# Attention and mixture of experts on one core: which unit the planner calls next, and how three quarters of the outputs are added up

## The chip, the core and the metric

The kernel runs on one core of one Trainium2 chip, and everything is float32. The time is the device time of one execution in microseconds (us). The kernel before took 654.52 us, the median of three runs (654.38 to 657.39). Engines are named as the profile names them: PE for matmuls (PEld for the loading of their weights), DVE, ACT, POOL and SP. Each has an in-order queue of its own.

## The reference, cut to what matters

The input x has 4 x 1024 tokens of 256 channels. The output is x plus two branches that both read the layer-normalised x:

```
xn = layernorm(x)
x + attention(xn) + ffn(xn)

# attention: 16 heads of 16 channels
local  = causal linear attention(q, k, v), chunks of 128 tokens
fine   = sum over 4 memories, weighted by a softmax over the batch's mean queries
coarse = one summed memory
memory = p * fine + (1 - p) * coarse          # p from a small gate on coarse
output = (gate * memory + (1 - gate) * local) @ w_o.T

# ffn: 8 experts of width 176, two for each token, and a shared one of width 352
scores = softmax(x @ gate_weight.T); the two largest, normalised
y = sum over the token's two experts of weight * (silu(x @ wg.T) * (x @ wu.T)) @ wd.T
y = y + shared(x)
```

## The kernel before

**Tiles.** The 4096 tokens are 32 tiles of 128 rows (`NTT` = 32), in blocks of 4 tiles (`NT` = 4). A *round* n does the attention of tile n on PE: `scores`, `memory`, `local`, `back`, `update`, `turned`, `gate_hidden`, and for tile n - 2 `output`, which adds the shared expert's second half and the projection by `w_o` in one PSUM bank. Beside the rounds run the projections and the shared expert of later blocks, and the routed experts: a sort of the tokens by expert fills 71 slot tiles (`NST` = 71) of 128 rows each. For each slot tile j, POOL gathers its rows from DRAM (`fetch_rows`, L1133, tile `xg`), SP loads the expert's weights (`fetch_weights`), PE transposes the rows (`expert_turn`, `pte`, L1166), does the two halves of the expert (`expert_hidden`, `phe`, L1183, and `expert_out`, `pye`, L1215), ACT scales the result (`expert_y`, tile `y`, L1224) and POOL scatters it with an adding indirect DMA (`put`, L1229) onto `sums`, an array in DRAM with a row for each token, which starts as a copy of x (L1615). Any `put` can touch any row, so each waits until the one before it has landed.

**The end of an output.** `held_from` is 24. For tiles 24 to 31, `output` comes last in the program: their rows of `sums` are loaded by `residual` (L1055), DVE adds them to the bank (`output_sum`, L1083), and ACT's queue stores them one at a time (`store_one`). For tiles 0 to 23, `output` comes in the rounds, ACT copies the bank to SBUF (`output_copy`, L1089, tile `acc`), and the rest waits for the last `put`: twelve loads of two tiles each from `sums` on SP's queue (`experts_part`, L1099, tile `part`), twelve additions on POOL (`total`, L1113) and twelve stores on SP's queue (`store_two`, L1117).

**The planner.** The order of the instructions is written by a list scheduler in the kernel's own Python (`plan`, L1357 on). It keeps a queue of units for each function, a table `cost` with each unit's engine and an assumed duration, `needs`, which names the units that one waits for, and `lag` and `landing`, the assumed time from a unit's end until its result can be used. It walks through time: of all units whose inputs are planned, each engine's candidate is the one that can begin first; the earliest over the engines is called next. On PE, among units that can begin equally early, the one that is due first goes:

```
            rank = (begin, due if engine == "PE" else ready)
```

`batch_weights` (L689 on) makes a softmax over the memories once for each of the four batches: two small matmuls (`pr`, L695), then some dozen short DVE instructions with one on ACT (L700 to L719). The table books it as 3.50 us of PE and nothing on DVE.

Of the kernel before, what the change touches and what calls it, by code (L numbers as in the profile page):

```python
# [8 lines left out]
FP = mybir.dt.float32  # L9
I32 = mybir.dt.int32  # L10
AF = mybir.ActivationFunctionType
ALU = mybir.AluOpType
AX = mybir.AxisListType

P = 128
NT = 4
TB = P * NT
# [5 lines left out]
def linear_attention_moe_kernel(  # L23
# [28 lines left out]
    nc = tc.nc  # L52
    T, H = x.shape
# [3 lines left out]
    NC = H // P  # L57
# [667 lines left out]
    def at(n):  # L725
        blk, i = divmod(n, NT)
        return blk, i, slice(i * P, (i + 1) * P)
# [360 lines left out]
        blk, i, _ = at(n)  # L1088
        nc.scalar.copy(st["acc", blk][:, i, :], st.pop(("po", n))[:, :H])  # L1089

    def experts_part(n):

        if n < 3 * NT:
            if n % NT == 0:
                st["parts"] = big.tile([P, NT, VW], FP, tag="tok", name=f"part_{n}")
            res = st["parts"][:, n % NT : n % NT + 2, :H]
        else:
            res = in_weights(n)
        nc.sync.dma_start(  # L1099
            res, sums[n * P : (n + 2) * P, :].rearrange("(n p) h -> p n h", p=P)  # L1100
        )
        st["part", n] = res

    def in_weights(n):
        tag, parts = ("wgu", [P, NC, 2, F]) if n % 4 else ("wdn", [P, 2, H])
        flat = "p a b c -> p (a b c)" if n % 4 else "p a b -> p (a b)"
        res = exw.tile(parts, FP, tag=tag, name=f"part_{n}").rearrange(flat)
        return res[:, : 2 * H].rearrange("p (n h) -> p n h", h=H)

    def total(n):  # L1110
        blk, i, _ = at(n)
        acc = st["acc", blk][:, i : i + 2, :]
        nc.gpsimd.tensor_add(acc, acc, st.pop(("part", n)))  # L1113

    def store(n, tiles, queue):
        blk, i, _ = at(n)
        queue.dma_start(  # L1117
            out[n * P : (n + tiles) * P, :].rearrange("(n p) h -> p n h", p=P),
            st["acc", blk][:, i : i + tiles, :],
        )  # L1120

    def store_two(n):
        store(n, 2, nc.sync)

    def store_one(n):
        store(n, 1, nc.scalar)


    def fetch_rows(j):
# [227 lines left out]
    def plan(order):  # L1357
# [12 lines left out]
            scores: ("PE", 1.10), memory: ("PE", 0.85), local: ("PE", 1.05), back: ("PE", 0.92),  # L1370
            update: ("PE", 0.48), turned: ("PE", 0.45), keys_back: ("PE", 0.45),
            output: ("PE", 2.17), gate_hidden: ("PE", 0.47), project: ("PE", 1.73),
            shared_gate: ("PE", 1.73), shared_up: ("PE", 1.73), batch_weights: ("PE", 3.50),
            expert_turn: ("PE", 0.24), expert_hidden: ("PE", 1.36), expert_out: ("PE", 0.95),
            odd_keys: ("ACT", 0.52), turned_copy: ("ACT", 0.57), keys_copy: ("ACT", 0.62),
            output_copy: ("ACT", 0.40), local_copy: ("ACT", 0.60), gate_out: ("ACT", 0.90),
# [3 lines left out]
            gate_sum: ("DVE", 0.50), blend: ("POOL", 0.78), weigh_local: ("DVE", 1.08),  # L1380
            state: ("DVE", 0.43), projected: ("DVE", 0.74), shared_silu: ("DVE", 0.66),
            shared_hidden: ("DVE", 0.66), expert_silu: ("DVE", 1.00), mean_queries: ("DVE", 1.30),
            gate_coarse: ("POOL", 0.78), sum_fine: ("POOL", 2.80), base: ("POOL", 0.78),
            add_state: ("POOL", 0.80), put: ("POOL", 1.62), fetch_rows: ("POOL", 1.02),
            fetch_weights: ("SP", 0.3), invert: ("DVE", 1.15), hold: ("ACT", 1.00),
            hold_weights: ("POOL", 0.72), add_slots: ("PE", 0.75), inverted: ("DVE", 0.65),
            residual: ("SP", 2.0), experts_part: ("SP", 1.0), output_sum: ("DVE", 0.45),
            total: ("POOL", 1.4), store_two: ("SP", 1.0), store_one: ("ACT", 0.1),
        }

        lag = {"PE": 0.22, "ACT": 0.06, "DVE": 0.06, "POOL": 0.06, "SP": 4.0}
        landing = {fetch_rows: 2.0, put: 2.9, residual: 2.5, experts_part: 2.5}
        batch = batches[1] - batches[0]

        def key_of(f, args):
# [2 lines left out]
        def needs(f, n, *more):  # L1398
# [8 lines left out]
                scores: lambda: qs + ks + [(odd_keys, n), (fine, n - 1, NC - 1)],  # L1407
                mask: lambda: [(scores, n), (local, n - 1)],
                memory: lambda: [(mask, n, g) for g in range(NG)],
                weigh: lambda: [(memory, n), (turned, n - 2), (gate_coarse, n - 1)],  # L1410
                gate_coarse: lambda: [(weigh, n), (base, n - 1), (sum_fine, n - 1)],
                fine: lambda: [(weigh, n), (sum_fine, n - 1)],
                sum_fine: lambda: [(fine, n, NC - 1), (gate_coarse, n), (gate_out, n - 2)],
# [20 lines left out]
                + [(shared_hidden, blk, f) for f in range(NF)],  # L1434
                output_copy: lambda: [(output, n)],
                output_sum: lambda: [(output, n), (residual, n - n % NT)],
                residual: lambda: [(put, NST - 1), (residual, n - NT)],
                experts_part: lambda: [(residual, NTT - NT)],
                total: lambda: [(experts_part, n), (output_copy, n), (output_copy, n + 1)],
                store_two: lambda: [(total, n)],  # L1440
                store_one: lambda: [(output_sum, n)],

                invert: lambda: [(add_slots, n - 3 * batch)],
                hold: lambda: [(invert, n), (add_slots, n - 3 * batch)],
# [28 lines left out]
                expert_silu: lambda: [(expert_tanh, n), (expert_out, n - 2)],  # L1473
                expert_out: lambda: [(expert_silu, n)],
                expert_y: lambda: [(expert_out, n), (put, n - 3)],
                put: lambda: [(expert_y, n), (put, n - 1)],
            }[f]()


# [22 lines left out]
        def longest_free(ring):  # L1502

            slots = [(-1.0 if u is None else called[u], k)
                     for k, u in enumerate(rings[ring]) if u is None or u in called]
            return min(slots)[1] if slots else None
# [3 lines left out]
        def add(f, args, due):  # L1510
            queues.setdefault(f, []).append((key_of(f, args), args, due, place))

        for w, f, *args in order:

            if f is end:
                ended = True
            if f not in cost:
                continue
            if not ended:
                place = due  # L1520
            add(f, args, due)
            if f is project:
                add(project_exp, [args[0], *args[2:]], due)
            elif f is fine and args[1] == NC - 1:
                add(sum_fine, args[:1], due)
            elif f is expert_turn:
                if args[0] + 2 < NST:
                    add(fetch_rows, [args[0] + 2], due)
                if args[0] + 1 < NST:
                    add(fetch_weights, [args[0] + 1], due)  # L1530
            if not (f is update and args[0] % (BPB * NT) == last_of_batch):
                for g in after.get(f, ()):
                    if f is output and args[1]:
                        g = output_sum
                    add(g, args[:1] if f is output else args, due)
            if cost[f][0] == "PE":
                due += cost[f][1]
        known = {op[0] for queue in queues.values() for op in queue}
        queues = {f: queue[::-1] for f, queue in queues.items()}
        free = dict.fromkeys(lag, 0.0)  # L1540
        done, called = {}, {}
        window = 12.0
        while any(queues.values()):
            limit = window + min(
                (q[-1][3] for f, q in queues.items() if q and cost[f][0] == "PE"), default=0.0
            )
            best = {}
            for f, queue in queues.items():
                if not queue:
                    continue  # L1550
                key, args, due, place = queue[-1]
                engine = cost[f][0]
                if engine == "PE" and place > limit:
                    continue
                waits = [key for key in needs(*key) if key in known]
                takes = taken(f, key)
                if takes:
                    slot = longest_free(takes[0])
                    if slot is None:
                        continue  # L1560
                    waits += [rings[takes[0]][slot]]
                if any(w is not None and w not in done for w in waits):
                    continue
                ready = max((done[w] for w in waits if w is not None), default=0.0)
                begin = max(ready, free[engine])
                rank = (begin, due if engine == "PE" else ready)
                if engine not in best or rank < best[engine][0]:
                    best[engine] = rank, f
            assert best
            rank, f = min(best.values(), key=lambda b: b[0][0])  # L1570
            begin = rank[0]
            key, args, *_ = queues[f].pop()
            engine, took = cost[f]
            takes = taken(f, key)
            if takes:
                rings[takes[0]][longest_free(takes[0])] = takes[1]
            called[key] = len(called)
            if f is update and (state, *key[1:]) not in known:
                took = 0.0
                done[add_state, *key[1:]] = begin  # L1580
                called[add_state, *key[1:]] = len(called)
            free[engine] = begin + took
            done[key] = begin + took + landing.get(f, lag[engine])
            f(*args)


# [91 lines left out]

    order += [(0, end)] + [u for n in range(last_round, NTT + 2) for u in rounds[n]]
    order += [(10, residual, n) for n in range(held_from, NTT, NT)]  # L1680
    order += [(10, experts_part, n) for n in range(0, held_from, 2)]
    for n in range(0, held_from, 2):
        order += [(64, total, n), (10, store_two, n)]
    order += [u for pair in shared(NBLK - 1) for u in pair if u]
    for n in range(held_from, NTT):
        order += [(1280, output, n, True), (10, store_one, n)]
    planned.append(True)
    plan(order)

# [55 lines left out]
```

## Time and profile before

The profiled execution took 651.07 us; the span from its first to its last instruction is 649.4 us.

| what | value |
|---|---|
| median of the runs, lowest and highest | 654.52, 654.38, 657.39 us |
| profiled execution, its span | 651.07, 649.4 us |
| granted PE clock, mean | 0.998 |
| busy share: PE, PEld, DVE, ACT, POOL | 97%, 75%, 66%, 43%, 63% |
| adding scatters, L1229: count, mean, share of POOL | 71, 1585 ns, 112.6 us |
| gathers of rows, L1133: count, mean | 71, 1006 ns |
| additions at the end, L1113: count, mean | 12, 1222 ns |

"Busy" is the time in which an engine's instructions were under way. A matmul is pipelined, so PE can be busy and still have small holes. A row of waits names the engine and line that waited, who released it, then the total, the number of times and the longest in us. In a timeline the columns are start, length, engine, line, operation, and in square brackets the engine's idle time before it with what ended it.

### The profile page before, as it was taken

To read this page: it belongs to the slowest core of one execution; us is meant where nothing else is said; L and a number is where in the kernel's file an instruction comes from. 1 tells how busy PE (TensorE), PEld (TensorE's weight loads), DVE (VectorE), ACT (ScalarE), POOL (GpSimd) and SP (SyncE) were. 2 spreads that over 40 slices of the span, in tenths; PEclk is the share of its full clock that TensorE was granted. 3 is DMA by queue.
4 is the path that set the end of the run, shared out by engine and by line. 5 is a ranking of instruction groups with operands and counts; after the bars stand their busy time and mean duration, and the time that the engine had idled before them with its cause. 6 is when DMAs were issued, how large, how long until landed. Compare 5 with 4: busy or idle time off the path is not lost.

```text
span 649.4 us, 15187 instructions
## 1 busy us (share of the span) xinstructions
PE 627.6 (97%) x5510; PEld 487.9 (75%) x5510; DVE 429.5 (66%) x1205; ACT 278.5 (43%) x676; POOL 408.6 (63%) x456
## 2 busy tenths in 40 slices
PE   4999999989999999999999999999999999999996
PEld 3884467778888877777786777788888886778775
DVE  6837999966665566566656765666655656667751
ACT  3765455444444454334533444333445434344320
POOL 5310055677777876565665665677777498586876
PEclk9999999999999999999999999999999999999999
DMA  9779000156566753443443444346666675564278
GB/s 301 242 238 248 0 1 2 50 168 166 133 152 144 164 129 87 106 107 77 109 118 78 106 107 98 89 106 138 154 151 160 149 161 127 147 164 99 26 225 301
DMA packets 94379, 86.51 MB, mean 133 GB/s; under 512 B 12033, under 2 KB 91905, under 8 KB 94177
## 3 DMA queue, kind: packets, MB, share of 16 engines
q1 hardware_dynamic: 78976, 65.34, 34.5%
q0 software_dynamic: 13632, 18.62, 16.6%
q10 hardware_dynamic: 1696, 1.58, 0.7%
q8 instruction: 44, 0.72, 0.5%
q14 instruction: 31, 0.25, 0.1%
HBM read 67.56 MB, written 23.59 MB: 140 GB/s over the span
## 4 chain that ended last, share of the span: by engine, by line
PE 89%; DVE 6%; ACT 1%; DMA 1%; issue 1%; POOL 0%; DVEq 0%
PE phe L1183 14%; PE pye L1215 11%; PE po L1071 6%; PE psu L1030 6%; PE pg L1010 5%; PE quad L746 5%; PE pn L772 5%; PE pv L407 5%; PE po L1075 4%; PE quad L889 4%; PE pq L649 3%; PE pk L649 3%; PE pte L1166 3%; PE pb L793 2%; PE pb L799 2%; PE found L617 2%
## 5 line engine op out<-in xcount | busy, mean ns | idle before, releaser
L1229 POOL DMA_INDIRECT sums<-y,islot x71 | 112.6, 1585 | 56.5 <-ACT y L1224 16.1
L1183 PEld LDWEIGHTS phe<-turned,wgu 128*128 128x128 f32 (+1 forms) x852 | 102.2, 187 | 14.9 <-issue 12.9
L1183 PE MATMUL phe<-turned,wgu 128*128 128x128 f32 (+1 forms) x852 | 108.0, 276 | 0.0
L1133 POOL DMA_INDIRECT xg<-xns,islot x71 | 71.4, 1006 | 58.0 <-PE pte L1166 43.9
L753 DVE TENSOR_TENSOR sT<-quad,causal 128x512 f32<-128x512 f32 x128 | 79.4, 682 | 21.9 <-PE quad L746 9.5
L1215 PE MATMUL pye<-wdn,hidden 112*128 112x256 f32 (+1 forms) x284 | 77.9, 396 | 0.5
L1200 DVE SCALAR_TENSOR_TENSOR the<-the,phe 128x256 f32<-128x256 f32 x71 | 29.5, 415 | 43.3 <-ACT the L1195 30.0
L1215 PEld LDWEIGHTS pye<-wdn,hidden 112*128 112x128 f32 (+1 forms) x284 | 48.8, 190 | 11.4 <-issue 3.2
L936 POOL TENSOR_TENSOR fm<-fm 128x512 f32<-128x512 f32 x32 | 48.2, 1506 | 4.2 <-DVE fm L923 4.2
L1224 ACT ACTIVATE y<-pye,wslot 128x256 f32<-128x256 f32 x71 | 33.4, 471 | 38.9 <-PE pye L1215 36.2
L1195 ACT ACTIVATE the<-phe 128x256 f32<-128x256 f32 x71 | 27.1, 382 | 51.6 <-PE phe L1183 45.8
L608 POOL TENSOR_TENSOR held<-ones,two 128x213 f32<-128x213 f32 (+1 forms) x22 | 16.3, 748 | 49.5 <-DVE ones L581 49.5
L1071 PE MATMUL po<-wd,h 128*128 128x256 f32 (+1 forms) x192 | 47.0, 380 | 0.0
L1010 PE MATMUL pg<-xnT,wg 128*128 128x512 f32 (+1 forms) x96 | 45.7, 598 | 0.5 <-DVE th L1040 0.5
L1030 PE MATMUL psu<-xnT,wu 128*128 128x512 f32 (+1 forms) x96 | 45.9, 600 | 0.0
L923 DVE TENSOR_TENSOR fm<-quad,rw 128x512 f32<-128x512 f32 x64 | 41.0, 682 | 0.2
L1071 PEld LDWEIGHTS po<-wd,h 128*128 128x128 f32 (+1 forms) x192 | 35.5, 190 | 6.1 <-issue 1.6
L916 POOL TENSOR_TENSOR cg<-coarse,gates 128x256 f32<-128x256 f32 x32 | 30.9, 964 | 13.9 <-DVE coarse L904 11.6
L1173 ACT COPY turned<-pte 128x256 f32<-128x256 f32 x71 | 26.5, 373 | 27.6 <-PE pte L1166 25.6
L1002 POOL TENSOR_TENSOR o<-o,loc 128x256 f32<-128x256 f32 x32 | 29.7, 929 | 7.8 <-ACT o L996 5.8
L772 PE MATMUL pn<-sT,va 128*32 128x128 f32 x1024 | 34.6, 276 | 0.0
L827 POOL TENSOR_TENSOR loc<-loc,cg 128x256 f32<-128x256 f32 x32 | 26.5, 827 | 12.7 <-DVE loc L817 12.0
(200 smaller groups left out, 1329.8 us busy)
## 6 DMA issues: line engine op xcount, KB each, us to landing
wdn<-in_w_down_dram SPq DMA_DIRECT2D x71, 224.0 KB
wgu<-in_w_gate_dram SPq DMA_DIRECT2D x71, 176.0 KB
wgu<-ups SPq DMA_DIRECT2D x71, 176.0 KB
xns<-x SPq DMA_DIRECT2D x8, 512.0 KB
sums<-in_x_dram SPq DMA_DIRECT2D x8, 512.0 KB
x<-in_x_dram SPq DMA_DIRECT2D x7, 512.0 KB
part<-sums SPq DMA_DIRECT2D x12, 256.0 KB
out_dram<-acc SPq DMA_DIRECT2D x12, 256.0 KB
```

The costliest lines, as they stand in the source:

```text
L649: nc.tensor.matmul(pq, w[:, k, c * P : (c + 1) * P], xnT[:, k, :], start=(k == 0), stop=(k == NC - 1),)
L753: nc.vector.tensor_mul(sT, quad[:, g, :].rearrange("p (c t) -> p c t", t=P), causal[:, None, :].to_broadcast([P, NC * 2, P]),)
L772: nc.tensor.matmul(pn[CW * r : CW * (r + 1), q, :], wide[:, i, first : first + CW], st["sT", h // 2][:, c * 2 + h % 2, :], start=True, sto ...
L923: nc.vector.tensor_mul(fm[:, c].rearrange("p g m (r k) -> p g (m r) k", k=HD), quad[:, :, c * KM + KX + KN : (c + 1) * KM].rearrange("p g ...
L936: nc.gpsimd.tensor_add(fm[:, :, 0:2, :], fm[:, :, 0:2, :], fm[:, :, 2:4, :])
L1010: nc.tensor.matmul(pg[:n, :], wg[:, k, f * P : f * P + n], xnT[:, k, :], start=(k == 0), stop=(k == NC - 1),)
L1030: nc.tensor.matmul(pu[:n, :], wu[:, k, f * P : f * P + n], xnT[:, k, :], start=(k == 0), stop=(k == NC - 1),)
L1071: nc.tensor.matmul(po[:, :H], st["h", blk, f][:k, tok], wd[:k, f, :], start=(f == 0), stop=False)
L1133: nc.gpsimd.indirect_dma_start(out=xg, out_offset=None, in_=xns, in_offset=bass.IndirectOffsetOnAxis(ap=islot[:, j : j + 1], axis=0),)
L1183: nc.tensor.matmul(ph[: cols.stop - cols.start, s, :], wgu[:, k].rearrange("p g f -> p (g f)")[:, cols], xgT[:, k, :], start=(k == 0), sto ...
L1215: nc.tensor.matmul(py[:, :H], hT[:n, f, :], wdn[:n, f, :], start=(f == 0), stop=(f == 1))
L1229: nc.gpsimd.indirect_dma_start(out=sums, out_offset=bass.IndirectOffsetOnAxis(ap=islot[:, j : j + 1], axis=0), in_=st.pop(("y", j)), in_of ...
```

## The change

The change has two parts, both in the functions above.

**The planner.** For PE, a unit is no longer ranked by when its inputs are planned to be ready, but by that time plus a margin by the engine that makes the input (`spare`: ACT 0.4, DVE 0.6, POOL 1.5, SP 1.0 us); the unit's due time decides among units that are past the margin. The time at which a unit is booked now counts all its inputs and the buffer that it takes. `batch_weights` is booked with 0.95 us of PE, and DVE is held for a further 2.2 us after it, and `weigh` waits for it. `sum_fine` is booked with 3.20 us rather than 2.80.

**The outputs of tiles 0 to 23.** `experts_part`, `in_weights`, `total` and `store_two` are gone. After each odd tile's `output_copy`, `join` adds two tiles of `acc` onto their rows of `sums` by one adding DMA of 256 KB from POOL's queue. It takes its turn with the `put`s, one landed before the next begins. After the last one, six copies of 512 KB from `sums` to `out` (`copy_out`, SP's queue, DRAM to DRAM) take the place of the twelve loads and twelve stores.

```diff
-    def experts_part(n):
...
-    def in_weights(n):
...
-    def total(n):
+    def join(n):
+
         blk, i, _ = at(n)
-        acc = st["acc", blk][:, i : i + 2, :]
-        nc.gpsimd.tensor_add(acc, acc, st.pop(("part", n)))
-
-    def store(n, tiles, queue):
+        nc.gpsimd.dma_start(
+            sums[n * P : (n + 2) * P, :].rearrange("(n p) h -> p n h", p=P),
+            st["acc", blk][:, i : i + 2, :],
+            accum_op=ALU.add,
+        )
+
+    def copy_out(blk):
+        rows = slice(blk * TB, (blk + 1) * TB)
+        nc.sync.dma_start(out[rows, :], sums[rows, :])
+
+    def store(n):
         blk, i, _ = at(n)
-        queue.dma_start(
-            out[n * P : (n + tiles) * P, :].rearrange("(n p) h -> p n h", p=P),
-            st["acc", blk][:, i : i + tiles, :],
-        )
-
-    def store_two(n):
-        store(n, 2, nc.sync)
-
-    def store_one(n):
-        store(n, 1, nc.scalar)
+        nc.scalar.dma_start(out[n * P : (n + 1) * P, :], st["acc", blk][:, i, :])
...
-            shared_gate: ("PE", 1.73), shared_up: ("PE", 1.73), batch_weights: ("PE", 3.50),
+            shared_gate: ("PE", 1.73), shared_up: ("PE", 1.73), batch_weights: ("PE", 0.95),
...
-            gate_coarse: ("POOL", 0.78), sum_fine: ("POOL", 2.80), base: ("POOL", 0.78),
+            gate_coarse: ("POOL", 0.78), sum_fine: ("POOL", 3.20), base: ("POOL", 0.78),
...
-            residual: ("SP", 2.0), experts_part: ("SP", 1.0), output_sum: ("DVE", 0.45),
-            total: ("POOL", 1.4), store_two: ("SP", 1.0), store_one: ("ACT", 0.1),
+            residual: ("SP", 2.0), copy_out: ("SP", 0.3), output_sum: ("DVE", 0.45),
+            join: ("POOL", 1.2), store: ("ACT", 0.1),
...
-        landing = {fetch_rows: 2.0, put: 2.9, residual: 2.5, experts_part: 2.5}
+        landing = {fetch_rows: 2.0, put: 2.9, join: 3.8, residual: 2.5}
...
-                weigh: lambda: [(memory, n), (turned, n - 2), (gate_coarse, n - 1)],
+                weigh: lambda: [
+                    (memory, n), (batch_weights, n // (BPB * NT)), (turned, n - 2), (gate_coarse, n - 1)
+                ],
...
-                put: lambda: [(expert_y, n), (put, n - 1)],
+                put: lambda: [(expert_y, n)],
...
+        serial = (put, join)
+        free = dict.fromkeys([*lag, "rows"], 0.0)
+        done, called, by = {}, {}, {}
+
+        spare = {"PE": 0.0, "ACT": 0.4, "DVE": 0.6, "POOL": 1.5, "SP": 1.0}
...
-                begin = max(ready, free[engine])
-                rank = (begin, due if engine == "PE" else ready)
+                begin = max(ready, free[engine], free["rows"] if f in serial else 0.0)
+                rank = (begin, ready)
+                if engine == "PE":
+                    safe = max((done[w] + by.get(w, 0.0) for w in waits if w), default=0.0)
+                    rank = (max(begin, safe), due)
...
             free[engine] = begin + took
+            if f in serial:
+                free["rows"] = begin + took + landing[f]
             done[key] = begin + took + landing.get(f, lag[engine])
+            by[key] = spare[engine]
+            if f is batch_weights:
+                free["DVE"] = max(free["DVE"], done[key]) + 2.2
+                done[key] = free["DVE"]
             f(*args)
...
     order += [(10, residual, n) for n in range(held_from, NTT, NT)]
-    order += [(10, experts_part, n) for n in range(0, held_from, 2)]
-    for n in range(0, held_from, 2):
-        order += [(64, total, n), (10, store_two, n)]
+    order += [(10, copy_out, blk) for blk in range(held_from // NT)]
```

## The prediction

> **What bounds the kernel now.** I read the page first, then the waits of PE, then the timeline where PE waits, and last the windows of the end.
>
> ```profile
> PE 627.6 (97%) x5510; PEld 487.9 (75%) x5510; DVE 429.5 (66%) x1205; ACT 278.5 (43%) x676; POOL 408.6 (63%) x456
> ...
> L1229 POOL DMA_INDIRECT sums<-y,islot x71 | 112.6, 1585 | 56.5 <-ACT y L1224 16.1
> ...
> L1133 POOL DMA_INDIRECT xg<-xns,islot x71 | 71.4, 1006 | 58.0 <-PE pte L1166 43.9
> ```
>
> PE is the bound: 97% of the span, and the chain that ended last is 89% PE. The change leaves every matmul as it is, so it can win only the time in which PE waits, and the time after PE's last matmul. The waits of PE:
>
> ```profile
> PE pt L385 <- ACT x L367: 8.7, 2, 7.6
> PE pb L793 <- ACT nT L784: 2.4, 2, 1.2
> PE pte L1166 <- DMA xg<-xns,islot: 2.2, 2, 1.4
> PE pte L1166 <- issue: 1.1, 1, 1.1
> PE pg L1010 <- DVE th L1040: 0.5, 1, 0.5
> PE pk L838 <- ACT oc L965: 0.3, 1, 0.3
> ```
>
> 8.7 us are the first load and normalisation, which the change doesn't touch. The rest, with two rows of 0.2 us, comes to 6.9 us in 640. Holes shorter than about 0.15 us aren't in this list. The Trainium skill ("Trainium Kernel Development and Optimization", Performance Expectations) calls matmul busy time a bad metric because matmuls are pipelined; so I don't take 6.9 us as all that could be won, and allow some 3 us more below the view's limit.
>
> The end, in windows (us, length, busy time of PE, PEld, DVE, ACT and POOL with instructions, granted clock, DMA share, GB/s):
>
> ```profile
> 625.00:635.00 10.00, 10.00 (x49) 8.40 (x48) 2.81 (x8) 1.38 (x4) 8.18 (x10) 1.00 1.09 352
> 635.00:645.00 10.00, 8.97 (x42) 7.53 (x40) 2.12 (x5) 0.00 (x0) 8.42 (x8) 1.00 1.08 379
> 645.00:650.00 5.00, 0.00 (x0) 0.00 (x0) 0.00 (x0) 0.00 (x0) 0.00 (x0) 0.68 0.26 91
> ```
>
> Two things fill these 20 us: PE without a hole, and the DMA engines, full at 352 to 379 GB/s. The last addition on DVE ends at 644.43 and the last store is issued at 644.73, so 4.6 us of the span lie behind that issue.
>
> **The end of the outputs.** Gone are 12 loads and 12 stores of 256 KB (6.3 MB) and the 12 additions (L1113, 14.2 us of POOL). None of it is on the path: PE is busy beside it to 644. The six copies move 3.1 MB. The trace has such copies: the eight of 512 KB that fill `sums` (L1615), in a window from 44 to 58 us with DMA share 1.00 at 316 GB/s. So 3.1 MB take about 10 us. They stand behind the two loads of residuals, which the last scatter releases at 621.5; 1 MB at 350 GB/s is 3 us, so they land near 635 to 636, nine us before the last store. They pass no instruction that anyone waits for: SP has nothing else left.
>
> What is won is only that the last 128 KB store finds free DMA engines. In the row of waits at the end SP waits 3.8 us for stores to land. How long one takes alone: the last scatter, as large, ends on POOL at 617.81 + 1.59 = 619.40, and SP's load that waits for its landing goes out at 621.51, so 2.1 us with the DMA share at 0.18. From 644.73 + 0.34 to about 648.6 the store took 3.5. The gain lies between 0 and 1.4; I take **0.8**, as a store's first bytes may be no earlier than the scatter's.
>
> **The joins.** Twelve adding DMAs go onto POOL between 134 and 600 us, where POOL is busy 324.6 of 466 us. The trace has none of this form. The gather (1006 ns, 128 rows of 1 KB, no addition) bounds the cost from below; twice the scatter (2 x 1585 = 3170 ns, for 256 rows) from above. The nearest row is the scatter, also an addition from SBUF to `sums`; the join has twice its rows but no indices. I take 1.6 us, so 12 x 1.6 = 19 us, and POOL goes from 70% to 74%. Behind a waiting join stand, in the order of the changed program, the next blend or gate (`o`, `cg`), whose transposes PE needs, and the next gather. The series of scatters: 71 x (1.59 + 2.1) = 262 us of the 472 between the first and the last; twelve joins of about 1.6 + 2.6 (landing scaled for twice the bytes) add 50, so the series has room. Cover is POOL's idle 30%; I cost the joins at nothing. Without cover a join costs PE what exceeds the planner's 1.2 us and its margin of 1.5.
>
> A rule speaks against them: "SBUF — State Buffer" (the box on "DVE blocks DMA") says that POOL cannot write its descriptors while DVE runs a two-port operation; a DMA of 620 ns then takes 3100. By it the joins would cost 12 x 3.1 = 37 us of POOL, and the excess over 2.7 would reach PE. The row decides: the 71 scatters take 1563 / 1586 / 1641 ns (lowest, median, highest) beside a DVE that is busy 64% of that stretch. Nothing there is blocked that way.
>
> **The planner.** The waits by cause:
>
> - *The softmax.* Timeline at 338 to 345:
>
> ```profile
> 338.09 0.22 DVE L700 COPY rel<-pr 128x64 f32<-128x64 f32 x1 [2.59 <-PE pr L695]
> ...
> 340.58 0.28 DVE L719 COPY w<-alive 128x8 f32<-128x8 f32 x1
> ...
> 343.48 0.41 DVE L1200 SCALAR_TENSOR_TENSOR the<-the,phe 128x256 f32<-128x256 f32 x1
> ...
> 344.62 0.41 PE L1166 MATMUL pte<-ident,xg 128*128 128x128 f32 x2 [1.07 <-issue]
> ```
>
> The softmax holds DVE from 338.09 to 340.86, 2.8 us that the old plan books on PE (3.5, against 0.5 measured) and not on DVE. So DVE comes to the expert's product (L1200) 2.7 us after ACT gave its input (340.40 + 0.38), and PE waits 1.1 us for a bank. With 2.2 us booked on DVE most of this goes: **-1.1**.
>
> - *nT to pb, 2.4 us.* By the order of the changed program and the rows' durations, the PE work between `local` and `back` of one tile goes from 1.32 to 1.72 us in the median (shortest: 0.90 to 1.19). 0.4 us more margin covers part. But in one case (ACT idle for 3.2 us before `nT` at 533.56, though PE's matmul had started at 530.1) the lateness isn't the plan's. I take half, **-1.2**.
>
> - *The first gathers, 2.2 us.* They get worse. From the last matmul of the sort (128.0) to the first transpose (134.16) it is 6.2 us. Before, an output, `memory`, `gate_hidden` and `local` lie between: 2.2 + 0.8 + 0.4 + 1.1 = 4.5 us. In the changed order only `scores`, `turned` and an output: 1.1 + 0.4 + 2.2 = 3.7. And `expert_hidden` of tile 0 follows straight on its transpose, so PE also waits for ACT's copy (0.37, about 0.7 with its signals); the second transpose then finds its rows there (0.8 won). In sum 0.8 + 0.7 - 0.8 = **+0.7**.
>
> - *The small ones*, 0.5 + 0.3 + 0.2 + 0.2 = 1.2 us: half goes, **-0.6**. And of the some 3 us below the view's limit a third, **-1.0**.
>
> What is late next is the same kind of thing at other places; the halves allow for that.
>
> **The sum.** -1.1 - 1.2 + 0.7 - 0.6 - 1.0 = -3.2, with the end -4.0 us. The profiled execution took 651.07 us, so its like would take 647.1. The median of the runs lies 3.45 us above it, which no view explains, and I leave that as it is: 654.5 - 4.0 = **650.5 us**. Since what can be told from no change is about 0.5%, 3.3 us, the limit is 651.2.
>
> **Rivals.**
>
> *More is won.* The margins take away nearly all listed waits but the first gathers (6.9 - 2.2 = 4.7), all 3 us below the limit, and the end gives 1.0: 654.5 - 8.7 + 0.7 = 646.5. For it: no unit pair in the changed order is closer than its chain needs, except the first expert. Against it: part of the waits isn't the plan's.
>
> *No change.* A new order moves waits rather than removing them; only the end's 0.8 stays: 653.7. For it: the plan's gaps differ from before in most rounds; the expert's two halves stand nearer (a tenth of them within 4.1 us of PE work, before 5.2). Against it: the softmax was booked wrongly, and now isn't.
>
> *Slower: POOL.* Place: the blends and gathers behind a join. If a join holds POOL for 3.2 us, it exceeds 1.2 + 1.5 = 2.7 by 0.5, and each of twelve delays PE by that: +6, so 654.5 - 4.0 + 6.0 = 656.5. It decides from about 2.7 us a join. For it: twice the rows, one landing to wait for, and tensor operations on POOL stretch already (L936 from 1.27 to 1.84 us). Against it: POOL's longest waits are its own, 43.9 us for PE at the gathers.
>
> That the change doesn't do what it says is ruled out: the program has 12 adding DMAs on POOL and 6 copies on SP, and as many matmuls as before.
>
> **How the numbers follow.** Forecast 0.42 (648 to 652.5), more won 0.14, no change 0.22, slower 0.22. Of the forecast's 0.42, 0.36 lie below 651.2. Faster 0.36 + 0.14 = 0.50, same 0.06 + 0.22 = 0.28, slower 0.22. The range goes from a little below the second case to a little above the slower one's 656.5: 645.5 to 657.
>
> **What would show it.** Right: PE's list without the 1.1 us of issue near 344 and with about 1.2 for `nT`; 2.5 to 3 us at the first `pte`; the join's row at 1.3 to 2 us; the DMA engines quiet from 636; under 4 us from the last store to the end. Wrong: a join over 2.7 us, PE waits on `o`, `cg` or `xg` just behind joins, or a sum of PE's waits that is no smaller while other names stand in it.

## The result, and the profile after

The changed kernel took 657.6 us in the median of 20 runs (654.26 to 660.66), the kernel before 654.45 beside it. The ratio is 1.0038, with a 95% interval of 1.0022 to 1.0054: a little slower, 7 us above the forecast of 650.5 and 0.6 us outside its range. Measured twice more (E9 and E13 below), the ratio was 1.0086 (1.0053 to 1.012) and 1.0032 (1.0016 to 1.0049). The profiled execution took 657.98 us with a span of 656.3 and a mean granted clock of 0.992.

The rows of the page that answer to those shown of before:

```profile
PE 630.9 (96%) x5510; PEld 489.2 (75%) x5510; DVE 432.0 (66%) x1205; ACT 278.8 (42%) x676; POOL 412.4 (63%) x456
...
L1209 POOL DMA_INDIRECT sums<-y,islot x71 | 112.8, 1588 | 58.4 <-DMA sums<-y,islot 14.4
...
L1113 POOL DMA_INDIRECT xg<-xns,islot x71 | 72.3, 1018 | 42.1 <-PE pte L1146 29.5
```

(From here on a line of the changed program is 20 lower than that of the same code before.) The same matmuls now keep PE busy for 630.9 us instead of 627.6, and the share falls from 97% to 96%: PE is slower *and* waits more. The waits of PE say where:

```profile
PE pt L385 <- ACT x L367: 9.1, 2, 8.0
PE pte L1146 <- DMA xg<-xns,islot: 3.8, 1, 3.8
PE pt L950 <- POOL o L1002: 3.1, 1, 3.1
PE po L1071 <- DVE hidden L1185: 1.6, 1, 1.6
PE phe L1163 <- PE pte L1146: 0.9, 1, 0.9
```

`nT` and the 1.1 us of issue near 344 are gone, as forecast. In their place stand two waits of over 3 us, each at one place. The windows around the two (columns as before; each ends where the granted clock can change, see below) show what comes with them:

```profile
136.01:139.43 3.42, 1.20 (x6) 0.71 (x4) 1.42 (x3) 0.37 (x1) 2.93 (x5) 1.00 0.57 168
139.43:142.84 3.41, 1.41 (x5) 1.04 (x6) 0.00 (x0) 0.37 (x1) 3.10 (x3) 0.50 0.40 115
142.84:146.25 3.41, 3.41 (x25) 3.08 (x27) 0.72 (x3) 0.76 (x2) 1.73 (x3) 0.50 0.81 118
231.59:235.00 3.41, 0.50 (x5) 0.50 (x6) 1.77 (x8) 0.35 (x1) 2.53 (x3) 1.00 0.64 138
235.00:238.40 3.40, 3.40 (x7) 1.32 (x6) 2.29 (x4) 0.58 (x1) 2.52 (x3) 0.50 0.66 145
```

The granted clock falls to 0.50 late: at 139.43, when PE has waited for 2.2 us and will wait for 1.5 more, and at 235.00, half a microsecond after the second wait has ended. It stays there for 6.8 and for 3.4 us, most of them full of work. In the profiled execution of before it was full from the warm-up to the last matmuls.

**The first gathers.** POOL's timeline, from the additions in front to the first gathers, then PE's:

```profile
133.34 1.27 POOL L936 TENSOR_TENSOR fm<-fm 128x512 f32<-128x512 f32 x1
...
136.90 0.72 POOL L827 TENSOR_TENSOR loc<-loc,cg 128x256 f32<-128x256 f32 x1
137.80 1.23 POOL L1113 DMA_INDIRECT xg<-xns,islot  x1 [0.18 <-issue]
```

```profile
132.95 0.41 PE L617 MATMUL found<-held,ones 128*128 128x142 f32 x2
...
136.18 1.03 PE L1075 MATMUL po<-wo,oc 128*128 128x256 f32 x4
140.97 0.66 PE L1146 MATMUL pte<-ident,xg 128*128 128x128 f32 x2 [3.77 <-DMA xg<-xns,islot]
142.09 2.93 PE L1163 MATMUL phe<-turned,wgu 128*128 128x128 f32 x12 [0.46 <-ACT turned L1153]
```

The same two places before:

```profile
127.76 0.41 PE L617 MATMUL found<-held,ones 128*128 128x142 f32 x2
...
134.16 0.41 PE L1166 MATMUL pte<-ident,xg 128*128 128x128 f32 x2 [1.44 <-DMA xg<-xns,islot]
```

DVE made `islot`, the row numbers that the gathers need, at 134.68 + 0.23 = 134.91, but in POOL's queue six additions stand ahead of the gather, from `o` at 132.66 to `loc`, and it starts 2.9 us later. From the sort's last matmul to the first transpose it is 8.0 us (140.97 - 132.95), before 6.4 (134.16 - 127.76). PE has 4.2 us of work in between. Then twelve matmuls of `phe` take 2.93 us; at full clock they take 1.49.

**The blend at 231 us.** POOL, then PE, then POOL's blend before:

```profile
225.70 1.59 POOL L1209 DMA_INDIRECT sums<-y,islot  x1 [0.25 <-issue]
...
230.79 1.59 POOL L1209 DMA_INDIRECT sums<-y,islot  x1 [0.31 <-issue]
232.68 1.01 POOL L1113 DMA_INDIRECT xg<-xns,islot  x1 [0.31 <-issue]
233.71 0.74 POOL L1002 TENSOR_TENSOR o<-o,loc 128x256 f32<-128x256 f32 x1
235.57 1.30 POOL L1094 DMA_DIRECT2D sums<-acc  x1 [1.13 <-DMA sums<-y,islot]
```

```profile
234.50 0.44 PE L950 MATMUL pt<-ident,o 128*128 128x128 f32 x2 [3.07 <-POOL o L1002]
...
234.99 3.58 PE L649 MATMUL pk<-xnT,wk 128*128 128x512 f32 x4
```

```profile
225.19 0.74 POOL L1002 TENSOR_TENSOR o<-o,loc 128x256 f32<-128x256 f32 x1
```

ACT delivered `o` at 226.73. POOL's blend of it starts at 233.71, behind three additions, a memset, a scatter and a gather. Before, the same blend came at 225.19 and PE did not wait. No join stands in this stretch of POOL's queue (the last one was issued at 197.74), so this trace alone doesn't say that the joins are the cause.

**The joins and the end.** A join takes 1300 / 1314 / 1392 ns of POOL (lowest, median, highest). How long a scatter takes to land in mid-kernel can be read where the next one waits for it, here in the trace of before:

```profile
210.16 1.58 POOL L1229 DMA_INDIRECT sums<-y,islot  x1 [2.03 <-DMA sums<-y,islot]
...
215.42 1.57 POOL L1229 DMA_INDIRECT sums<-y,islot  x1 [0.90 <-DMA sums<-y,islot]
```

The first landed 5.26 - 1.58 = 3.7 us after its end on POOL. The end of the changed kernel in windows:

```profile
635.00:645.00 10.00, 10.00 (x52) 8.81 (x51) 2.65 (x8) 2.03 (x6) 2.44 (x4) 1.00 1.00 371
645.00:650.00 5.00, 5.00 (x25) 4.38 (x24) 0.85 (x2) 0.00 (x0) 0.00 (x0) 1.00 0.20 71
```

The DMA engines are full while the six copies run and nearly idle from 645 on, 8 us before PE's last matmul, which ends at 653.2. From PE's last matmul to the end it is 3.2 us, before 5.4.

### The profile page after: what moved, and what is told of

Same layout as the page of the kernel before. It is cut to its first block, busy times and chain, and to the rows that moved or that the text cites. A ratio compares the mean times of both kernels' runs of the same rounds, so it can differ in the third digit from the quotient of the medians.

```text
span 656.3 us, 15167 instructions
## 1 busy us (share of the span) xinstructions
PE 630.9 (96%) x5510; PEld 489.2 (75%) x5510; DVE 432.0 (66%) x1205; ACT 278.8 (42%) x676; POOL 412.4 (63%) x456
## 3 DMA queue, kind: packets, MB, share of 16 engines
q10 hardware_dynamic: 1696, 1.58, 0.7%
## 4 chain that ended last, share of the span: by engine, by line
PE 83%; DVE 9%; POOL 2%; ACT 2%; issue 2%; DMA 1%; another core or an unknown queue 0%; DVEq 0%; POOLq 0%; ACTq 0%
PE phe L1163 14%; PE pye L1195 10%; PE po L1071 6%; PE psu L1030 5%; PE pg L1010 5%; PE quad L746 5%; PE pv L407 5%; PE pn L772 4%; PE po L1075 4%; PE quad L889 3%; PE pk L649 3%; PE pq L649 3%; PE pte L1146 2%; PE found L617 2%; PE pt L950 2%
## 5 line engine op out<-in xcount | busy, mean ns | idle before, releaser
L1163 PE MATMUL phe<-turned,wgu 128*128 128x128 f32 (+1 forms) x852 | 109.7, 279 | 1.4 <-PE pte L1146 0.9
L916 POOL TENSOR_TENSOR cg<-coarse,gates 128x256 f32<-128x256 f32 x32 | 27.4, 855 | 15.7 <-DVE coarse L904 11.6
L827 POOL TENSOR_TENSOR loc<-loc,cg 128x256 f32<-128x256 f32 x32 | 30.0, 937 | 6.1 <-DVE loc L817 5.5
```

The source lines that it names most:

```text
L1163: nc.tensor.matmul(ph[: cols.stop - cols.start, s, :], wgu[:, k].rearrange("p g f -> p (g f)")[:, cols], xgT[:, k, :], start=(k == 0), sto ...
```

## The experiments

Ratios are to the kernel before, measured in the same call; in brackets the 95% interval. Chips and hours differ by some us (the kernel before had medians from 651.5 to 655.7 us), so times are compared only within a call.

**E1 to E4: which half of the change makes which wait?** E1 is the changed planner with the old outputs; E2 the old planner with the joins and copies; E3 leaves the plan and drops the calls; E4 widens the planner's view.

```diff
# E3, in plan:
-            f(*args)
+            if f is not join:
+                f(*args)
# E4, in plan:
-            limit = window + min(
+            limit = (window if (expert_turn, 0) in called else 24.0) + min(
```

> The changed planner alone, with the outputs as they were before (loads, additions and stores at the end, no joins). Theory 'margins': the new rank itself leaves PE without work at the first gathers (its own plan has a gap of 2.96 us before the first expert's transpose, the old plan has none), and a PE wait of over 3 us halves the granted clock for some us. Then the wait of 3 to 4 us at the first pte and a stretch of half clock are here too, worth about 6 us; the wait for o at 231 us is absent or under 1.5, since no join crowds the scatters; the end takes 5.4 us after PE as before. With the 3 to 4 us won elsewhere: 656 to 658 (before 654.5). Rival 'joins': without joins neither of the two long waits is here, and the planner's gain shows: 650 to 652.

> The joins and the copies alone, with the planner of before (old rank, no margins, old costs; a join takes its turn with the scatters in the plan). Theory 'margins': no wait over 2 us at the first pte, no half clock; the end is shorter by 2.2 us; the joins cost PE nothing: 651.5 to 653.5. Rival 'joins': the twelve joins, each 1.3 us of POOL and a place in the series of landings, delay blends and gathers; PE waits of 3 us for o or xg: 656 to 660.

> The changed kernel with its plan and order kept, but the twelve joins not issued (the additions of the outputs of tiles 0 to 23 are left out). Theory 'margins': the wait at the first pte stays at 3.5 to 4 us with its half clock, so the kernel stays within 1 us of the changed one on that account. At 231 us two versions are open: if the scatters' landings alone hold POOL's queue, the wait of 3 us for o stays (655.5 to 657.5); if the joins push the scatters back, it goes with its half clock, 4.7 us (651.5 to 653). Rival 'joins': both waits go, 646 to 648.

> The changed kernel with one edit: until the first expert's transpose is planned, the planner may look 24 us ahead on PE instead of 12. In its plan the gap of 2.96 us before the first transpose is gone. Theory 'margins': the wait at the first pte falls under 1 us, no half clock near 140 us, about 6 us are won there; what comes at 231 us depends on the new order, so 646 to 652. Rival 'joins' or 'the gathers are simply late': the wait stays at 3 to 4 us whatever PE has to do before it, 656 to 658.

| | ratio | half clock in the profile |
|---|---|---|
| E1 planner alone | 1.0040 (1.0025 to 1.0054) | 6.8 us at the first gathers |
| E2 outputs alone | 1.0101 (1.0067 to 1.0136) | 3.4 us each at 231, 532 and 570 |
| E3 no joins | 0.9993 (0.9981 to 1.0006) | 6.8 us at the first gathers |
| E4 wider view | 1.0044 (1.0028 to 1.0061) | 3.4 us each at 143 and 235 |

The waits of E1:

```profile
PE pte L1166 <- DMA xg<-xns,islot: 3.8, 1, 3.8
PE quad L889 <- DVE sT L753: 1.5, 2, 0.8
```

The wait at the first gathers is here without any join, and no `o` is in the list. The waits of E2:

```profile
PE pt L950 <- POOL o L1002: 4.7, 3, 3.2
PE pye L1195 <- issue: 3.1, 1, 3.1
PE pt L950 <- DVE loc L817: 1.8, 1, 1.8
PE pte L1146 <- DMA xg<-xns,islot: 2.2, 2, 1.6
```

Here it is the other way round: the first gathers are as before, and blends are late. So neither theory holds alone. The planner makes the first wait without any join, and the joins make blends late without the new planner. E2's POOL shows one way:

```profile
524.28 1.01 POOL L1113 DMA_INDIRECT xg<-xns,islot  x1 [0.30 <-issue]
527.44 1.30 POOL L1094 DMA_DIRECT2D sums<-acc  x1 [2.15 <-DMA sums<-y,islot]
528.26 1.24 POOL L916 TENSOR_TENSOR cg<-coarse,gates 128x256 f32<-128x256 f32 x1
528.95 1.23 POOL L1002 TENSOR_TENSOR o<-o,loc 128x256 f32<-128x256 f32 x1
```

The join stands idle for 2.15 us until the scatter before it (issued at 522.41, done on POOL at 523.98) has landed, and `cg` and `o` stand behind the join. E3 agrees: in the same order without joins the wait for `o` is gone and the ratio is 0.45% (2.9 us) lower than that of the changed kernel, which was measured in another call; the first gathers stay. The two profiles differ in more than the joins, though: in E3 POOL's blend comes 1.4 us earlier (232.35), and PE reaches this place 2.2 us later. The clock of all executions says more (3.4 us at half take 0.0026 off its mean): it is 0.994 or higher in all 22 of E3, and 0.992 or lower in 23 of the 45 of the changed kernel in its three measurements. E4 was a miss: the wait at `pte` is gone, but a wait of 2.6 us for `nT`, whose release the trace doesn't name, takes its place, and the clock is halved all the same.

**E5, E6, E11: the clock and the order.** E5 puts matmuls that nothing needs into both waits, E11 only into the first. E6 moves one scatter.

```diff
# E5 and E11, in expert_turn:
+        for _ in range(34 if j == 0 else 0):
+            nc.tensor.transpose(pt[:, 0, :], ident, ident)
# E5 also, in turned:
+        for _ in range(28 if n == 6 else 0):
+            nc.tensor.transpose(pt[:, 0, 0, :], ident, ident)
# E6, at the end of plan, with the calls kept in a list:
+        late = calls.pop(names.index((put, 13)))
+        calls.insert(names.index((blend, 6)), late)
```

> The changed kernel with matmuls that nothing needs put into the two long waits of PE: 34 transposes of the identity ahead of the first expert's (about 3.7 us at 110 ns) and 28 ahead of tile 6's own (about 3.1 us). Order and arrival of everything else stay. Theory 'the idle PE costs its clock': no stretch of half clock remains near 140 and 235 us, although rows and o arrive as late as before; 6.8 + 3.4 us of half clock are 5.1 us of work, so 651.5 to 653 against 657 for the changed kernel. Rival 'the half clock comes from elsewhere, or costs nothing': the half clock stays, 656 to 658.

> The changed kernel with one scatter (of slot tile 13) moved behind the blend of tile 6 on POOL's queue; all twelve joins stay, PE's order stays. Theory 'the series in POOL's queue': that scatter waits for the landing of the one before it and holds the gather and the blend behind it; moved away, the wait of 3.1 us for o at 231 us is under 1 us, its half clock goes too, and 4 to 5 us are won: 652 to 653.5. Rival 'POOL's time': the joins and stretched additions make POOL late by their durations, and the wait only shrinks by the scatter's 1.6 us: 655 to 656.

> The changed kernel with 34 transposes that nothing needs ahead of the first expert's alone. The rows arrive as late as before. If a long idle stretch of PE costs its clock, 6.8 us of half clock near 140 us go, 3.4 us of work, so the time is 2.5 to 4 us below the changed kernel of the same call. If the half clock is without effect or has another cause: within 1 us of it.

E5's PE at the first gathers:

```profile
138.21 3.87 PE L1148 MATMUL pte<-ident 128*128 128x128 f32 x34
142.01 0.44 PE L1150 MATMUL pte<-ident,xg 128*128 128x128 f32 x2
142.91 1.59 PE L1167 MATMUL phe<-turned,wgu 128*128 128x128 f32 x12 [0.46 <-ACT turned L1157]
```

The rows come as late as ever, but `phe` takes 1.59 us instead of 2.93, and neither half-clock stretch is left: an idle PE had lost its clock. In time it is less clear. E5 gave 1.0032 (1.0018 to 1.0047), without the changed kernel in its call. E11 gave 1.0072 (1.0045 to 1.0099) beside 1.0086 for the changed kernel (E9), 656.21 against 656.69 us: the clock was saved, and the time is what was expected if it had no effect. Both missed what was expected of the theory. E5 was therefore repeated beside the changed kernel:

> The changed kernel once more, as the measure for the three beside it on one chip: a ratio to the kernel before of 1.003 to 1.009, between its two earlier ones.

> The kernel with both long waits of PE filled by transposes, again, now with the changed kernel on the same chip. If the half clock costs what its length says (10.2 us at half, 5.1 us of work in the profiled execution, less in executions where the second wait is short and the filling is in the way), it is 2 to 5 us faster than the changed kernel. If the half clock costs nothing: within 1 us.

E13 took 658.3 us (ratio 1.0032), E14 656.4 (1.0022; 1.0009 to 1.0035). The medians differ by 1.9 us, but the intervals of the ratios overlap. The expected 5.1 us counted the whole 10.2 us at half rate as work. PE idles in 2.0 of them (the rest of the first wait, and the wait for `turned`), so at most 8.2 us of work, 4.1 us of loss, lie there. The halved rate is shown; that it costs more than some 2 us of a typical execution is not.

E6 missed too: 1.0088 (1.0072 to 1.0104). The wait for `o` shrank to 0.4 us, but the next one came 20 us later:

```profile
252.31 1.58 POOL L1209 DMA_INDIRECT sums<-y,islot  x1 [1.23 <-DMA sums<-y,islot]
253.35 1.30 POOL L1002 TENSOR_TENSOR o<-o,loc 128x256 f32<-128x256 f32 x1
```

Again a scatter waits for a landing, and a blend stands behind it; PE's transposes of that `o` waited 2.7 us, and 3.4 us at half clock followed. So it isn't one misplaced scatter.

**E9 and E10: POOL's time or the series?** E10 lets the joins add onto an array of their own (six copies that the changed kernel doesn't have fill it with x at the start; they are left out below).

```diff
-            sums[n * P : (n + 2) * P, :].rearrange("(n p) h -> p n h", p=P),
+            aside[n * P : (n + 2) * P, :].rearrange("(n p) h -> p n h", p=P),
```

> The changed kernel itself, unaltered, beside the three below on one chip. A ratio to the kernel before of 1.002 to 1.006, as in its first measurement; two stretches of half clock near 140 and 235 us, the second not in every execution, since the mean clock of its runs lies at 0.992 in some and 0.995 in others.

> The changed kernel with its plan kept, but the joins add onto an array of their own rather than onto the sums, so no join waits for a scatter and no scatter for a join (the outputs of tiles 0 to 23 are then missing from the result). POOL still issues all twelve. Theory 'the series of landings': the wait of 3 us for o at 231 us goes, as it did without joins; the wait at the first pte stays: 2 to 4 us below the changed kernel of the same call. Rival 'POOL's time': a join's 1.3 us and the additions stretched beside it delay the blend, so the wait for o stays over 2 us, and the time is within 1 us of the changed kernel.

E9: 656.69 us, 1.0086 (1.0053 to 1.012; six runs). E10: 653.77 us, 1.0041 (1.0021 to 1.0062), so 2.9 us less, as much as E3 won by leaving the joins out; the two intervals just touch. The join's 1.3 us on POOL are still there; what went is its place in the series. But E10's profiled execution, the slowest of its 16, still shows a wait of 3.1 us for `o`, with the scatters alone in the series, 4.5 to 6.0 us apart. So a long wait for `o` can come without a join in the series. The clock is 0.992 or lower in 5 of E10's 16 executions, in 5 of E9's 6, and in none of E3's 22. By its time E10 speaks for the series, but some part of the joins' 1.3 us on POOL isn't ruled out.

**E7, E12, E15, E16: the plan's own gap.** The changed planner's bookings can be read off: between the sort's last matmul and the first expert's transpose they hold 2.96 us in which PE has nothing, where the old planner's hold none. The margin of 1.5 us on POOL's results makes PE put off the sort's own matmuls (`add_slots`, which wait for POOL's `hold_weights`) behind other work; when they are done, the work within the planner's view of 12 us is used up, and too little is left to cover the gathers. E7 takes the margin off the two units that feed the sort.

```diff
-            by[key] = spare[engine]
+            by[key] = 0.0 if f is hold_weights or f is hold else spare[engine]
```

> The changed kernel with the margin taken from the sort's two units that feed its matmuls (hold on ACT, hold_weights on POOL), all other margins kept. In its plan the gap before the first expert's transpose is gone. Theory 'margins': the wait at the first pte is under 1.5 us, no half clock near 140 us, 5 to 6 us won there; the place at 231 us (joins) may stay or move: 651 to 653 if it stays, 646 to 648 if it goes. Rival 'the gathers are late whatever the order' : 656 to 658.

> The version without the sort's margin once more: a ratio to the kernel before of 0.990 to 0.994, mean clock 1.000 in every execution. If its first result was one chip's: 0.995 to 1.000.

> The changed planner without the margin on the sort's two units, and the outputs as before (no joins): the counterpart of the version without the sort's margin that has the joins (ratio 0.992). If joins and copies are worth what the end shows and cost PE nothing, this one is slower by 2 us (ratio 0.994 to 0.996). If the joins still cost as much in the rounds as they save at the end: ratio 0.990 to 0.993.

> The version without the sort's margin, with one part of the change undone: the softmax over the memories booked as before, 3.50 us of PE and none of DVE. If the booking is worth the 1.1 us of the prediction's sum, the wait of 1.1 us near 340 us comes back and it is 1 to 1.5 us slower than the version it is made from (about 648.5 where that takes 647). If a new order moves more than the booking does: another sign or size, with waits of other names.

E7: 647.13 us, **0.9918** (0.9902 to 0.9934), and E15 on another chip 0.9922 (0.9896 to 0.9948). It beats both kernels, with all twelve joins in it, and no row of its list of PE's waits, nor of E15's, names `o`. Its PE at the first gathers:

```profile
127.84 0.41 PE L617 MATMUL found<-held,ones 128*128 128x142 f32 x2
128.08 1.46 PE L1071 MATMUL po<-wd,h 128*128 128x256 f32 x6
...
131.72 1.08 PE L772 MATMUL pn<-sT,va 128*32 128x128 f32 x32
132.73 0.73 PE L860 MATMUL pu<-va,sk 128*128 128x136 f32 x4
133.95 0.41 PE L1146 MATMUL pte<-ident,xg 128*128 128x128 f32 x2 [0.49 <-DMA xg<-xns,islot]
```

The sort ends 5 us earlier, an output, `memory`, `gate_hidden`, `local` and `update` lie behind it, and PE waits 0.49 us. No stretch of half clock is left before the last matmuls. E12, the same planner with the old outputs, gave 0.9955 (0.9938 to 0.9972). E16, E7 with the softmax booked as before, took 656.11 us beside E15's 650.26: 5.9 us more, not the 1.1 to 1.5 expected, since `o` (3.7 us) and `sT` (3.1 us) now wait elsewhere and 6.8 us at half clock follow. What a booking is worth isn't the wait that it names, but the order that comes of it.

The two halves of the change in one table of ratios:

| planner | old outputs | joins and copies |
|---|---|---|
| before | 1 | 1.0101 |
| changed | 1.0040 | 1.0038, 1.0086, 1.0032 |
| changed, no margin on the sort | 0.9955 | 0.9918, 0.9922 |

**E8: the outputs without the series.** E7's planner; each pair of outputs is stored straight to the result, and at the end adding copies put the sums on top (the stores and the bookings are left out below).

```diff
-        nc.sync.dma_start(out[rows, :], sums[rows, :])
+        to, src = (t[rows, :].rearrange("(n p) h -> p n h", p=P) for t in (out, sums))
+        nc.gpsimd.dma_start(to, src, accum_op=ALU.add)
```

> As the one with the sort's margin taken away, and the joins replaced: each pair of outputs is stored straight to its rows of the result from ACT's queue, so it takes no place among the scatters, and the six copies at the end become six adding copies from the sums onto the result, from POOL's queue. Theory 'margins and series': neither long wait is left, no half clock, 646 to 649, provided that the adding copies land before the last store[...]. Rival 'the end gets longer': the adding copies move slower than that, and the end takes 10 us more: 655 to 660.

1.0069 (1.0053 to 1.0085): the rival. Its end in windows:

```profile
632.00:642.00 10.00, 7.66 (x36) 6.37 (x34) 1.70 (x4) 0.00 (x0) 4.79 (x4) 1.00 1.19 203
642.00:655.00 13.00, 0.00 (x0) 0.00 (x0) 0.00 (x0) 0.00 (x0) 0.00 (x0) 0.50 0.79 134
```

PE is done by 640, and the adding copies run on to 654.7: in the two windows all DMA together, with shares of 1.19 and 0.79, brings 203 and 134 GB/s, where it brought 371 beside the plain copies.

## Why the prediction was wrong, by its own steps

Two terms failed: the first gathers, which were mis-sized, and the joins, which were put at nothing. Follow the two profiled executions at equal work done by PE (an estimate: each kind of matmul is counted with its usual time before). The changed kernel is 0.8 us ahead when the sort ends, 5.1 us behind at 150 us, 9.6 behind after the blend at 231 us and 9.1 when PE is done. The end gives 2.2 back, and 6.9 remain, which is the difference of the two executions.

- **The first gathers, +0.7: the step that cost most.** The mechanism was right, and the size was wrong. From 0.8 ahead to 5.1 behind are 5.9 us. Without joins, taking the margin off the sort changes the ratio from 1.0040 (E1) to 0.9955 (E12, another call), 5.6 us. The chain from the sort to the first transpose was taken from the kernel before (6.4 us, start to start). It is 8.0, because the margin puts the sort's last matmuls 5 us later, and by then six additions stand in POOL's queue ahead of the gathers; in E7 the sort is early, and they are not in the way. The wait is 3.77 + 0.46 us instead of 2.9, and is long enough to halve the clock, which the sum had at nothing. The Trainium skill ("TensorE: Matmul & The Clock Gate", section "Why this matters for your kernels") warns of idle gaps of more than about 3 us between matmuls; the waits of 3.77 and 3.07 us agree, those of 1.6 us too, and a wait of 1.84 us in E2 that was also followed by 3.4 us at half rate shows that it is no sharp limit. That rule stood against this change, and the prediction didn't weigh it.
- **"The series has room" and "I cost the joins at nothing".** A scatter's landing was taken as 2.1 us, from the last one. (The DMA share of 0.18 named with it is the mean from 600 to 620; in the 2.1 us themselves it was 0.54.) In mid-kernel it is longer. At the seven places before where the series waited for a scatter's landing, it took 2.6 to 4.2 us (median 3.8); at thirteen in the changed kernel 2.4 to 4.4 (median 3.3). At 1.6 + 3.3 to 1.6 + 3.8 us a step, 71 scatters would fill 348 to 383 of the 472 us, not 262, and twelve joins at 1.3 + 3.3 us another 55. That is an estimate of 85 to 93% where the prediction had 66%. POOL's queue is in order, so whoever waits there holds the blends. The price is 2.9 us in the changed order (E10 against E9; E3), and 1.0% in the old planner's order (E2, six runs). But a full series isn't the whole cause: E7 has the same 83 members in 471 us, and its PE doesn't wait for `o`. Whether a late landing reaches PE depends on what PE has to do meanwhile, and the record doesn't show at what fill that begins to matter. The "slower" case had the place right (blends behind a join), but priced it by POOL's time, and a join of 1.31 us, under the 1.6 taken, never came near its threshold of 2.7.
- **The softmax, -1.1, and `nT`, -1.2.** Both waits went. But E16 shows that the first term can't be read so.
- **The end, -0.8.** Right in kind, too small: the profiles' ends differ by 2.2 us, and E7 against E12, from two calls, by 0.37%, 2.4 us. The bound of 1.4, taken from how long one scatter lands alone, did not hold. The copies landed at about 645, not 636: SP issued the residual loads at 631, not 621, since the last scatter came 10 us later.
- **The base.** The 3.45 us between the profiled execution and the median, "which no view explains", have a cause in part. The profiled execution had a mean clock of 0.998, and what it lacks lies behind PE's last matmul. In the 56 runs of the kernel before beside E13 the median clock was 0.994, and time rises as the clock falls (correlation -0.58, 0.4 us for each 0.001, so some 1.5 of the 3.45 us). So the typical execution of before has lost clock as well, and a profile with none of it understates what a better order can win: E7's clock is 1.000 in each of its six runs. Where before loses it, no kept trace shows.
- **The sum.** Of the planner's -3.2, E12 shows -2.9 once the sort has no margin, and E7 shows -0.8% (5.3 us) for the whole change, where -4.0 us were forecast. That the total then comes out near doesn't show that its single terms were right.

Open remain the half clock's share in the time (E13 and E14), the release of E4's `nT`, why E7's order has room for the joins and the changed one not, and why the changed kernel's ratio was 1.0086 in one call.

## What to carry to other kernels

A queue that is in order and holds instructions which wait for landings is full well before its engine is (here an estimated 85 to 93% of the series, with POOL busy 63%): count the series in steps, with the landing as it is in mid-kernel, not as it is when the memory is quiet. A margin in a scheduler also delays the units that start a long chain, and the chain then arrives when the work that should cover it is used up; look in the plan itself for the gap, before looking at the chip. Compare the granted clock of the profiled execution with that of the other runs before building a forecast on one profile.

## What was not expected of the hardware

The granted clock changes on a grid of 3.413 us. In the changed kernel's trace it changes at 139.43, 146.25, 235.00 and 238.41, which lie 2, 26 and 1 such steps apart. The windows shown above are steps of this grid, and what counts is how much of a step PE is busy, not how long a wait is. The steps in which PE was busy for 1.20, 1.41 and 0.50 us (35, 41 and 15%) were each followed by a step at half clock. E2's wait of 1.84 us fell into a step with 46% (528.57 to 531.98), and half clock followed. The wait of 1.6 us at 516.27 in the changed kernel fell into one with 53% (514.89 to 518.30), and none followed. Between 60 and 638 us of all eighteen traces, every step at full clock with less than 47% was followed by half clock and none with more than 54%; in between both occur. So the same wait can cost the clock in one execution and not in the next, as the grid falls. Before, the two waits at the first gathers (1.44 and 0.75 us) would leave PE 36% busy in a step that began at 132.7; whether its slower executions lose clock there isn't shown. The same skill page (Part 1, "What's actually happening") gives a free-running window of 3.4 us over which activity is judged, which the grid agrees with.

An adding DMA of 256 KB with 256 rows from SBUF takes less of POOL (1.31 us) than an adding scatter of 128 rows (1.59). And beside adding copies from DRAM to DRAM (E8) the DMA engines move 134 to 203 GB/s, where they move 371 beside plain ones.
